# A convolution over 256 positions as products of 32-point transforms, eight graphs at a time, in a graph layer on one Trainium2 core

## The chip, the core and the metric

The kernel runs on one core of a Trainium2 chip. The time is device time in microseconds (us), the median of several runs. The core's engines work side by side, each through its own list of instructions in order: TensorE (PE), which multiplies matrices into PSUM, VectorE (DVE), ScalarE (ACT), GpSimd (POOL) and SyncE (SP). SP does nothing here but issue transfers (DMA) between device memory and the on-chip memory SBUF. An instruction whose operands another engine makes waits for it on a semaphore, and everything behind it on its engine waits too.

## The reference

There are 64 graphs of 256 nodes with 256 channels, all in fp32. With `h = relu(layernorm(x))` as its input, the layer computes:

```
xc = transpose(h)                                  # channels x nodes
c  = relu(bn1(conv1d(xc, conv1_w, pad 0)))         # 256 -> 256 channels, one tap
c  = bn2(conv1d(c, conv2_w, pad 8))                # 256 -> 256 channels, 17 taps along the nodes
x_conv = transpose(relu(c + xc))
s = h @ w_se.T + b_se                              # 3 numbers a node
A = exp(-squared distance of the s) * adj          # 256 x 256 a graph
x_nmp = A @ relu(h @ w_msg.T + b_msg)
r, z = sigmoid of sums of [x_conv, x_nmp] @ w_ih and h @ w_hh
n = tanh(gi_n + r * gh_n)
out = x + (1 - z) * n + z * h
```

Of all matmul work, conv2 with its 17 taps is the largest piece, and the gates (`w_ih`, `w_hh`) come second.

## The kernel before

The loop runs over 32 groups of `G` = 2 graphs. Channels lie on the 128 partitions (two halves, `DC` = 2), and the 512 nodes of a group along the free dimension. For each group, `norm` normalises on DVE (with a power on POOL), `transpose_h` turns the result on PE and ACT writes the relu `HT`. `conv1` multiplies, and ACT writes `H1`. `embed`, `message` and `affinity` make the adjacency part; POOL multiplies the exponential with `adj` (L324). `transpose_a` and `aggregate` follow, then `gates` for each half of the channels (`dc`), with four sums in PSUM, and `finish` transposes back, adds x and stores.

Conv2 is done in a short fast form along the nodes: `points` evaluates the input at seven points on DVE, `conv2` multiplies with filters that were evaluated at the same points at the start (seven points, five or four terms, 68 matmuls of 128x128 for each half of the output), and DVE puts four outputs together from the sums (L295 to L307). The node order in SBUF is chosen so that the pieces are contiguous.

The order is written out by hand in the loop at the end (`manual_schedule`): each engine takes its instructions in the order in which the code issues them. Buffers come from pools; a tile with `bufs=1` is written again only when all its readers are done. PSUM has eight buffers of 128x512: four `aux`, four `acc`. All loads and stores in the loop go through SP.

Of the kernel before, what the change touches and what calls it, by code (L numbers as in the profile page):

```python
# [1 line left out]

# [11 lines left out]
BN_EPS = 1e-5  # L14


@with_exitstack
def kernel(
# [30 lines left out]
    NP = B // G  # L49
# [16 lines left out]

    const = ctx.enter_context(tc.tile_pool(name="const", bufs=1))
    loads = ctx.enter_context(tc.tile_pool(name="loads", bufs=2))
    psum = ctx.enter_context(tc.tile_pool(name="psum", bufs=4, space=bass.MemoryType.PSUM))
# [4 lines left out]
    def rows(t, i, h):  # L74
        return t[G * i:G * i + G].rearrange("g (k h c) d -> h k g (c d)", c=MC, h=2)[h]
# [9 lines left out]
    X, ADJ = {}, {}  # L85

    def load(i):
        X[i] = loads.tile([P, G * MC, D], FP, name="x", bufs=3)
        ADJ[i] = loads.tile([P, G * MC, N], FP, name="adj")
        for t, src in ((X[i], x), (ADJ[i], adj)):  # L90
            for h in range(2):
                nc.sync.dma_start(out=t[h * NK:(h + 1) * NK].rearrange("k (g c) d -> k g (c d)", g=G),
                                  in_=rows(src, i, h))

    load(0)


# [11 lines left out]
    def fold_bn(params, name):  # L109
# [7 lines left out]
        nc.vector.tensor_sub(shift, b, shift)  # L117
        return scale, shift

    w_c1 = const.tile([P, DC, D], FP)  # L120
    nc.scalar.dma_start(out=w_c1, in_=c1_wT.rearrange("(k p) o -> p k o", p=P))
# [9 lines left out]
    nc.scalar.dma_start(out=w_msg, in_=msg_wT.rearrange("(k p) o -> p k o", p=P))  # L131
    b_msg = const.tile([P, D], FP)
    nc.gpsimd.dma_start(out=b_msg, in_=bass.AP(tensor=msg_b.tensor, offset=msg_b.offset, ap=[[0, P], [1, D]]))
    stage_ctx = ExitStack()
    stage = stage_ctx.enter_context(tc.tile_pool(name="stage", bufs=1))
    w_c2 = stage.tile([P, DC, TAPS, D], FP)
    for k in range(DC):
        nc.scalar.dma_start(out=w_c2[:, k], in_=c2_wT[k * P:(k + 1) * P])

    w_pt = const.tile([P, 2 * len(PTS), DC, L, D], FP)  # L140
    w_inf = const.tile([P, DC, L - 1, D], FP)
    for k in range(DC):
        taps = w_c2[:, k, :(L - 1) * F, :].rearrange("p (l j) o -> p j l o", j=F)
        nc.scalar.copy(w_inf[:, k], taps[:, F - 1])
        for q, a in enumerate(PTS):
            norm_a = 2 * a
            for b in PTS:
                if b != a:
                    norm_a *= a * a - b * b
            ev = stage.tile([P, L - 1, D], FP, name="ev", bufs=2)  # L150
            od = stage.tile([P, L - 1, D], FP, name="od", bufs=2)
            nc.vector.scalar_tensor_tensor(ev, taps[:, 2], a * a, taps[:, 0], op0=ALU.mult, op1=ALU.add)
            nc.vector.scalar_tensor_tensor(od, taps[:, 3], a * a, taps[:, 1], op0=ALU.mult, op1=ALU.add)
            nc.scalar.mul(ev, ev, 1.0 / norm_a)
            nc.scalar.mul(od, od, a / norm_a)
            nc.vector.tensor_add(w_pt[:, 2 * q, k, :L - 1, :], ev, od)
            nc.vector.tensor_sub(w_pt[:, 2 * q + 1, k, :L - 1, :], od, ev)
            nc.scalar.mul(w_pt[:, 2 * q, k, L - 1, :], w_c2[:, k, TAPS - 1, :], 1.0 / norm_a)
            nc.scalar.mul(w_pt[:, 2 * q + 1, k, L - 1, :], w_c2[:, k, TAPS - 1, :], -1.0 / norm_a)
    stage_ctx.close()  # L160
    work = ctx.enter_context(tc.tile_pool(name="work", bufs=1, reuse_waits="tile"))
# [4 lines left out]
    s2, h2_shift = fold_bn(bn2, "bn2")  # L166
# [3 lines left out]
    nc.vector.tensor_scalar(b_rz, b_rz, 0.5, None, ALU.mult)  # L170


    LD = const.tile([P, W], FP, name="ld")
    RD = const.tile([P, W], FP, name="rd")
    nc.vector.memset(LD, 0.0)
    nc.vector.memset(RD, 0.0)
    nc.vector.memset(LD[64:64 + SE, :], -1.0)
    nc.vector.memset(RD[32:32 + SE, :], -1.0)

    H1 = const.tile([P, F, DC * G, EK], FP, name="h1")  # L180
    nc.gpsimd.memset(H1, 0.0)
# [286 lines left out]
```

## Time and profile before

| | us |
|---|---|
| median of 3 runs | 2827.28 |
| lowest, highest | 2826.51, 2827.72 |
| the profiled execution's own time | 2828.4 |
| its span, from first to last instruction | 2826.6 |
| mean granted clock of PE, share of full speed | 0.958 |

The profile is of one execution. Its span is what the views divide; 1.8 us of that execution's time lie outside it. Busy time is the time in which an engine had an instruction running. The chain that ended last is followed back from the last instruction, at each step to what released it. [...] An fp32 matmul shows as two instructions, and a transpose as one.

### The profile page before, as it was taken

The numbers are of one execution on the slowest core, as the hardware profiler recorded it, in microseconds if no ns is written. First come the engines' busy times: TensorE is split into PE (matmuls) and PEld (weight loads), VectorE is DVE, ScalarE is ACT, GpSimd is POOL, SyncE is SP. The second block draws the span as 40 slices with busy tenths as digits, with TensorE's granted clock in tenths as the row PEclk, the third lists the DMA queues.
The fourth block names the chain that finished last, engine by engine and source line by source line (L and its number), as shares of the span: only waits on it lengthen the run. The fifth ranks groups of instructions, "written<-read, shape, count | busy, mean of one in ns | idle before, by whom it ended". The sixth has DMA issues, their size and how long they took to land.

```text
span 2826.6 us, 31684 instructions
## 1 busy us (share of the span) xinstructions
PE 2589.7 (92%) x13440; PEld 1863.1 (66%) x13440; DVE 965.5 (34%) x2343; ACT 538.8 (19%) x923; POOL 348.3 (12%) x443
## 2 busy tenths in 40 slices
PE   0899999999999999999999999999999999999998
PEld 0676667766677766677766677766677766677665
DVE  4332432332323433323433323333323323323322
ACT  2112211112211112111122111122111122111121
POOL 2111001111011111011111011111011111011110
PEclk9899999999999999999999999999999999999998
DMA  4000000000000000000000000000000000000000
GB/s 143 8 23 0 23 23 23 23 17 7 23 23 23 23 8 16 23 23 23 23 1 23 23 23 23 23 1 23 23 23 23 23 1 23 23 23 23 8 1 15
DMA packets 29982, 59.87 MB, mean 21 GB/s; under 512 B 3696, under 2 KB 4208, under 8 KB 29584
## 3 DMA queue, kind: packets, MB, share of 16 engines
q1 hardware_dynamic: 27648, 50.34, 6.5%
q10 hardware_dynamic: 1632, 7.34, 0.8%
q8 instruction: 106, 1.74, 0.3%
q0 software_dynamic: 560, 0.16, 0.0%
q14 instruction: 36, 0.29, 0.0%
HBM read 41.05 MB, written 16.78 MB: 20 GB/s over the span
## 4 chain that ended last, share of the span: by engine, by line
PE 89%; DVE 4%; ACT 2%; issue 1%; POOL 0%; DMA 0%; ACTq 0%; DVEq 0%
PE acc L359 35%; PE acc L284 34%; PE aux L344 7%; PE acc L219 4%; PE aux L268 4%; DVE u L304 2%; PE aux L318 2%; PE aux L254 2%; ACT hT L213 1%; PE aux L388 1%; DVE u L307 1%; ACT aT L336 1%; ACT mb L292 0%; DVE u L306 0%; DVE sm L297 0%
## 5 line engine op out<-in xcount | busy, mean ns | idle before, releaser
L284 PE MATMUL acc<-xp,w_pt 128*128 128x128 f32 x7680 | 869.6, 274 | 0.0
L284 PEld LDWEIGHTS acc<-xp,w_pt 128*128 128x128 f32 x7680 | 866.9, 191 | 1.8
L359 PE MATMUL acc<-xnm,w_ih 128*128 128x512 f32 x768 | 360.9, 592 | 0.0
L359 PE MATMUL acc<-xcv,w_ih 128*128 128x512 f32 x768 | 360.9, 592 | 0.0
L359 PE MATMUL acc<-hT,w_hh 128*128 128x512 f32 x768 | 350.4, 592 | 0.0
L344 PE MATMUL aux<-aT,msg 128*128 128x256 f32 x512 | 199.5, 572 | 149.1 <-ACT aT L336 149.1
L378 POOL TENSOR_TENSOR d<-hT,nn 128x512 f32<-128x512 f32 x64 | 82.3, 1286 | 1592.7 <-ACT nn L372 1592.7
L344 PEld LDWEIGHTS aux<-aT,msg 128*128 128x128 f32 x512 | 151.7, 304 | 191.6 <-ACT aT L336 156.6
L359 PEld LDWEIGHTS acc<-xcv,w_ih 128*128 128x128 f32 x768 | 145.9, 190 | 183.7 <-issue 183.7
L359 PEld LDWEIGHTS acc<-xnm,w_ih 128*128 128x128 f32 x768 | 145.9, 190 | 183.7 <-issue 183.7
L359 PEld LDWEIGHTS acc<-hT,w_hh 128*128 128x128 f32 x768 | 145.9, 190 | 170.0 <-issue 160.7
L368 DVE SCALAR_TENSOR_TENSOR gn<-tr,gn 128x512 f32<-128x512 f32 x64 | 44.1, 689 | 521.9 <-ACT tr L367 521.9
L379 DVE SCALAR_TENSOR_TENSOR d<-tz,d 128x512 f32<-128x512 f32 x64 | 44.3, 692 | 340.6 <-ACT tz L375 340.6
L295 DVE TENSOR_TENSOR sm<-acc,ma 128x256 f32<-128x256 f32 x64 | 27.2, 425 | 347.2 <-ACT ma L291 347.2
L297 DVE TENSOR_TENSOR sm<-acc,mb 128x128 f32<-128x128 f32 x64 | 18.7, 292 | 351.8 <-ACT mb L292 351.8
L284 PE MATMUL acc<-xp,w_inf 128*128 128x128 f32 x1024 | 124.8, 273 | 0.0
L272 POOL TENSOR_SCALAR msg<-msg 128x512 f32<-128x512 f32 x64 | 95.1, 1487 | 232.6 <-DVE msg L271 229.8
L324 POOL TENSOR_TENSOR a<-e,adj 128x128 f32<-128x128 f32 x256 | 123.5, 518 | 0.6 <-ACT e L321 0.6
L284 PEld LDWEIGHTS acc<-xp,w_inf 128*128 128x128 f32 x1024 | 119.5, 191 | 0.0
L219 PE MATMUL acc<-hT,w_c 128*128 128x512 f32 x256 | 117.1, 601 | 0.0
L268 PEld LDWEIGHTS aux<-w_msg,hT 128*128 128x128 f32 x512 | 97.3, 190 | 28.5 <-issue 16.9
L268 PE MATMUL aux<-w_msg,hT 128*128 128x256 f32 x512 | 115.7, 379 | 0.0
(89 smaller groups left out, 1921.3 us busy)
## 6 DMA issues: line engine op xcount, KB each, us to landing
x<-in_x_dram SPq DMA_DIRECT2D x64, 256.0 KB, 4.1
adj<-in_adj_dram SPq DMA_DIRECT2D x64, 256.0 KB, 4.8
out_dram<-y SPq DMA_DIRECT2D x64, 256.0 KB, 4.7
w_c<-in_c_wT_dram ACTq DMA_DIRECT2D x2, 2176.0 KB, 14.8
w_ih<-in_ih_wT_dram ACTq DMA_DIRECT2D x1, 1536.0 KB, 6.6
w_hh<-in_hh_wT_dram ACTq DMA_DIRECT2D x1, 768.0 KB, 8.4
w_c<-in_c_wT_dram ACTq DMA_DIRECT2D x1, 256.0 KB, 2.6
w_msg<-in_msg_wT_dram ACTq DMA_DIRECT2D x1, 256.0 KB, 6.0
```

What stands on the lines that cost most here:

```text
L219: nc.tensor.matmul(p, w_c1[:, k, o * P:(o + 1) * P], HT[i][:, k, :], start=(k == 0), stop=(k == DC - 1))
L254: nc.tensor.matmul(p[:KD, :], w_se[:, k, :], HT[i][:, k, :], start=(k == 0), stop=(k == DC - 1))
L268: nc.tensor.matmul(p[:, c * D:(c + 1) * D], chunk(HT[i][:, k], g, c), w_msg[:, k, :], start=(k == 0), stop=(k == DC - 1))
L272: nc.gpsimd.tensor_relu(MSG[i][:, g], MSG[i][:, g])
L284: nc.tensor.matmul(p, w[:, o * P:(o + 1) * P], XP[i][:, q, k * G:(k + 1) * G, l:l + NK], start=(l == 0 and k == 0), stop=(l == last - 1 an ...
L304: nc.vector.scalar_tensor_tensor(u[:, r // 2, r % 2], t[:, q], PTS[q] ** r, t[:, 0] if q == 1 else u[:, r // 2, r % 2], op0=ALU.mult, op1= ...
L318: nc.tensor.matmul(p[:, c * N:(c + 1) * N], chunk(LD[:KD], g, c), graph(RD[:KD], g), start=True, stop=True)
L324: nc.gpsimd.tensor_mul(AF_[i][:, g, c, b * P:(b + 1) * P].rearrange("p (h k) -> p h k", h=2), e[:, c, b * P:(b + 1) * P].rearrange("p (h k ...
L344: nc.tensor.matmul(graph(p, g), MSG[i][:, g, c, dc * P:(dc + 1) * P], AT[i][:, g, c, :], start=(c == 0), stop=(c == MC - 1))
L359: nc.tensor.matmul(p, w[:, row:row + P], r, start=(j == 0), stop=(j == len(terms) - 1))
L378: nc.gpsimd.tensor_sub(d, HT[i][:, dc, :], nn)
L379: nc.vector.scalar_tensor_tensor(d, tz, 1.0, d, op0=ALU.add, op1=ALU.mult)
```

## The change

Conv2 is computed through real transforms of 32 points, for `GB` = 8 graphs at a time (`PB` = 4 groups), in eight rounds.

The 256 nodes are cut into 16 windows of 16, and each output window needs the two neighbouring input windows. `split` forms sums (`U`) and differences (`V`) of them on DVE. The class `Fft` lists the steps of the transforms: `odd` on V, `even` on U. The way back is `odd_back`, `q_back`, `p_back` and `join`. A step is one DVE instruction on 256 to 2048 elements per partition, mostly in pieces of 16 elements; 20 small scalings go to ACT. The transforms leave 16 bins. For each bin `products` does three real products in place of a complex one (the last bin needs two): 4 matmuls of 128x128 each. Two bins go together, into three PSUM buffers, and DVE combines them into `Yv` or `Yu` (L562, L563).

The steps wait in a list, `queue`. `pump(us)` issues steps from it until an assumed length is used up, `drain` issues all that is left; the calls stand between the other parts of the loop and so set DVE's order.

The filters' transforms are computed at the start with the same steps, on DVE, one half of the input channels after the other, and written to device memory (`filt`, 16 bins of 768 KB, 512 KB for the last). Each round reads all of them again through SP into `wb`, which has three buffers.

Around it: `adj` now has one buffer; x is loaded a second time (`y`) through POOL, which also stores; DVE takes the product with `adj` (L617) and the subtraction that stood at L378; ACT takes relu and scalings of `message` and `embed`; PSUM has three `aux` and five `acc`. `gates` first adds what does not need conv2, then calls `middle`, then adds conv2's part. `residual` adds `HT` to all four groups' results ahead of the first gate's second part.

The core of the diff:

```diff
+    def odd(self, V, T, S):
...
+        q = [self.sub(T(None, 0, 2), V(None, 6, 2), V(None, 2, 2)),
+             self.add(T(None, 2, 2), V(None, 6, 2), V(None, 2, 2)),
+             self.stt(V(None, 6, 2), T(None, 0, 2), -R2, V(None, 4, 2)),
+             self.stt(V(None, 2, 2), T(None, 2, 2), -R2, V(None, 0, 2)),
+             self.stt(V(None, 4, 2), T(None, 0, 2), R2, V(None, 4, 2)),
+             self.stt(V(None, 0, 2), T(None, 2, 2), R2, V(None, 0, 2))]
...
+    def load_adj(i):
+        ADJ[i] = work.tile([P, G * MC, N], FP, name="adj")
+        load_rows(ADJ[i], adj, i, nc.sync)
...
+    filt = dram.tile([BINS, P, 3, DC, D], FP, name="filt")
+    def put(bins, kind, k, t):
+        nc.sync.dma_start(out=filt[bins:bins + t.shape[1], :, kind, k, :].rearrange("n p o -> p n o"), in_=t)
...
+        for s in fft.odd(V, T, Sv):
+            s()
+        for c in range(2):
+            put(c * 4, 0, k, V(c, 4, 4)[:, 0])
...
+        return psum.tile([P, W], FP, name="acc", bufs=5)
...
+    queue = deque()
+    def pump(us):
+        while queue and us > 0:
+            us -= queue.popleft()() / 960.0 + 0.1
+    def drain():
+        pump(1e9)
...
+    def split(j):
+        hv = h1.rearrange("p a (c h) b -> p (a c) h b", c=2)
+        A = slice(2 * G * j * DC, 2 * G * (j + 1) * DC)
+        for s, b in ((4, 0), (0, 1)):
+            a, bb = hv[:, :, s:s + 4, b:b + NW], hv[:, :, s:s + 4, b + 1:b + 1 + NW]
+            nc.vector.tensor_sub(V(None, s, 4)[:, A], a, bb)
+            nc.vector.tensor_add(U(None, s, 4)[:, A], a, bb)
...
+    def load_bin(b, n):
+        b, n = b + n // BINS, n % BINS
+        if b < NB:
+            WB[b, n] = work.tile([P, 3, DC, D], FP, name="wb", bufs=3)
+            kinds = 3 if n < BINS - 1 else 2
+            nc.sync.dma_start(out=WB[b, n][:, :kinds], in_=filt[n, :, :kinds])
...
+    def products(b, m):
+        load_bin(b, 2 * m + 2)
+        p = [acc() for _ in range(3)]
+        for n in range(2):
+            for kind, v in enumerate(operands(2 * m + n)):
+                if v is None:
+                    continue
+                for o in range(DC):
+                    for k in range(DC):
+                        nc.tensor.matmul(p[kind][:, (n * DC + o) * P:(n * DC + o + 1) * P],
+                                         WB[b, 2 * m + n][:, kind, k, o * P:(o + 1) * P],
+                                         v[:, k::DC, 0, :], start=(k == 0), stop=(k == DC - 1))
+        load_bin(b, 2 * m + 3)
+        p1 = work.tile([P, W], FP, name="p1")
+        pv = [t.rearrange("p (n a e) -> p a n e", n=2, e=NW) for t in (p1, p[1], p[2])]
+        if m < 7:
+            nc.scalar.copy(p1, p[0])
...
+            nc.vector.tensor_sub(re, pv[0], pv[2])
+            nc.vector.tensor_add(im, pv[0], pv[1])
...
+    def residual(i):
+        for o in range(DC):
+            v = xcv(i % PB, o)
+            nc.vector.scalar_tensor_tensor(v, v, s2[:, o:o + 1], HT[i][:, o, :], op0=ALU.mult, op1=ALU.add)
+            nc.scalar.activation(v, v, AF.Relu, bias=h2_shift[:, o:o + 1])
...
-    def conv2(i, o):
...
-        nc.scalar.activation(XCV[i][:, o, :], uf, AF.Relu, bias=h2_shift[:, o:o + 1])
...
+        for g in range(G):
             for c in range(MC):
-                for b in range(MC):
-                    nc.gpsimd.tensor_mul(AF_[i][:, g, c, b * P:(b + 1) * P].rearrange("p (h k) -> p h k", h=2),
-                                         e[:, c, b * P:(b + 1) * P].rearrange("p (h k) -> p h k", h=2),
-                                         ADJ[i][:, g * MC + c].rearrange("p (k h c) -> p c h k", h=2, c=MC)[:, b])
+                e = E[i][:, g, c].rearrange("p (c h b) -> p c h b", c=MC, b=NW)
+                nc.vector.tensor_mul(e, e, ADJ[i][:, g * MC + c].rearrange("p (b h c) -> p c h b", c=MC, b=NW))
+        if i + 1 < B // G:
+            load_adj(i + 1)
...
+    def gates(i, dc, middle=None):
...
+        pr, pn, pz = acc(), acc(), acc()
+        product(pr, h + xn, r, True, False)
+        product(pn, xn, n, True, False)
+        product(pz, h + xn, z, True, False)
+        if middle:
+            middle()
+        product(pr, xc, r, False, True)
         tr = work.tile([P, W], FP, name="tr")
         nc.scalar.activation(tr, pr, AF.Tanh, bias=b_rz[:, dc:dc + 1], scale=0.5)
         nc.vector.scalar_tensor_tensor(gn, tr, 1.0, gn, op0=ALU.add, op1=ALU.mult)
-        pn = product(xi, 2 * D + dc * P)
+        pump(1.5)
+        product(pn, xc, n, False, True)
...
+    def prepare(b, j, stats=True):
+        if b < NB:
+            i = b * PB + j
+            if stats:
+                norm(i)
+            transpose_h(i)
+            conv1(i)
+            split(j)
+            if i + 2 < B // G:
+                load_x(i + 2)
...
+    for b in range(NB):
+        i = b * PB
+        if b == 0:
+            queue.extend(fft.odd(V, T, Sv))
+            drain()
+            queue.extend(fft.even(U, PT, T))
+        products(b, 0)
+        pump(4)
         embed(i)
         message(i)
+        products(b, 1)
+        pump(5)
         affinity(i)
-        if i + 2 < NP:
-            load(i + 2)
-        conv2(i, 0)
-        if i > 0:
+        if b > 0:
             finish(i - 1)
-        if i + 1 < NP:
-            norm(i + 1)
-        conv2(i, 1)
-        if i + 1 < NP:
-            transpose_h(i + 1)
+        products(b, 2)
+        pump(6)
         transpose_a(i)
+        products(b, 3)
+        drain()
+        queue.extend(fft.odd_back(Yv, T))
         aggregate(i)
-        gates(i, 0)
-        if i + 1 < NP:
-            conv1(i + 1)
-            points(i + 1)
+        products(b, 4)
+        pump(6)
+        embed(i + 1)
+        message(i + 1)
+        products(b, 5)
+        pump(5)
+        affinity(i + 1)
+        queue.extend(fft.q_back(Yu, T))
+        products(b, 6)
+        pump(8)
+        if b + 1 < NB:
+            norm(i + PB)
+        transpose_a(i + 1)
+        products(b, 7)
+        queue.extend(fft.p_back(Yu, T))
+        queue.extend(fft.join(Yu, Yv, T))
+        aggregate(i + 1)
+        pump(8)
+        if b + 1 < NB:
+            transpose_h(i + PB)
+        embed(i + 2)
+        message(i + 2)
+        pump(5)
+        affinity(i + 2)
+        drain()
+        for j in range(PB):
+            residual(i + j)
+        def more(b=b, i=i):
+            if b + 1 < NB:
+                conv1(i + PB)
+                split(0)
+                if i + PB + 2 < B // G:
+                    load_x(i + PB + 2)
+            transpose_a(i + 2)
+        gates(i, 0, more)
         gates(i, 1)
-    finish(NP - 1)
+        aggregate(i + 2)
+        prepare(b + 1, 1)
+        gates(i + 1, 0)
+        embed(i + 3)
+        message(i + 3)
+        prepare(b + 1, 2)
+        finish(i)
+        gates(i + 1, 1)
+        affinity(i + 3)
+        gates(i + 2, 0)
+        transpose_a(i + 3)
+        prepare(b + 1, 3)
+        if b + 1 < NB:
+            queue.extend(fft.odd(V, T, Sv))
+            even = fft.even(U, PT, T)
+            queue.extend(even)
+        finish(i + 1)
+        gates(i + 2, 1)
+        aggregate(i + 3)
+        gates(i + 3, 0)
+        finish(i + 2)
+        gates(i + 3, 1)
+        while b + 1 < NB and len(queue) > len(even):
+            queue.popleft()()
```

Three places where the order of instructions matters. The first is DVE at the beginning of a round (from the second round on). Before, `message` was followed by conv2's sums:

```order
L271 TENSOR_TENSOR msg<-aux,b_msg 128x256 x4
L295 TENSOR_TENSOR sm<-acc,ma 128x256
L296 TENSOR_TENSOR df<-acc,ma 128x256
L297 TENSOR_TENSOR sm<-acc,mb 128x128
L298 TENSOR_TENSOR df<-acc,mb 128x128
```

Now the last odd step (into Sv) stands ahead of the first products' sums, and even steps (PT, U, T) stand between these, `message` and the product with `adj`:

```order
L62 TENSOR_TENSOR Sv<-V 128x2048
L562 TENSOR_TENSOR Yv<-p_1891,acc 128x16x32
L563 TENSOR_TENSOR Yv<-p_1891,acc 128x16x32
L62 TENSOR_TENSOR PT<-U 128x2048
L65 TENSOR_TENSOR U<-U 128x32x64
L602 TENSOR_TENSOR msg<-aux,b_msg 128x256 x4
L562 TENSOR_TENSOR Yv<-p_1952,acc 128x16x32
L563 TENSOR_TENSOR Yv<-p_1952,acc 128x16x32
```

The first of these rows is what PE's first products of the round read. The second place is SP. Before, its list in the loop held only x, `adj` and the output of a group:

```order
L92 DMA x_1535<-in_x_dram 64x2x512 x2
L92 DMA adj_1536<-in_adj_dram 64x2x512 x2
L393 DMA out_0_dram<-y_1634 64x2x512 x2
L92 DMA x_1943<-in_x_dram 64x2x512 x2
L92 DMA adj_1944<-in_adj_dram 64x2x512 x2
```

Now, at the beginning of the second round, it holds bins 2 to 5, the next `adj`, then bins 6 and 7:

```order
L522 DMA wb_1860<-filt_138 128x1536
L522 DMA wb_1889<-filt_138 128x1536
L522 DMA wb_1921<-filt_138 128x1536
L522 DMA wb_1950<-filt_138 128x1536
L303 DMA adj_1976<-in_adj_dram 128x1x512 x2
L522 DMA wb_1996<-filt_138 128x1536
L522 DMA wb_2025<-filt_138 128x1536
```

Bins 6 and 7 feed the fourth products, and the load of `adj` ahead of them waits until DVE has read the buffer. The third place is ACT at the first gate of a round. Before, conv2's last activation (`xcv`) stood some rows ahead of the gates:

```order
L308 ACTIVATE xcv<-u,bn_shift 128x512
L213 ACTIVATE hT<-aux 128x512 x2
L336 COPY aT<-aux 128x512 x2
L346 ACTIVATE xnm<-aux 128x512 x2
L364 ACTIVATE gn<-acc,b_hh 128x512
```

Now eight residual activations stand directly ahead of the gate's first read of PSUM, `gn`, and of conv1 for the next round:

```order
L580 ACTIVATE Yv_76<-Yv_76,bn2_shift_376 128x512 x8
L658 ACTIVATE gn_1243<-acc_1240,b_hh_385 128x512
L500 ACTIVATE h1_398<-acc_1258,bn1_shift_125,bn1_scale_124 128x2x16x16
L500 ACTIVATE h1_398<-acc_1262,bn1_shift_125,bn1_scale_124 128x2x16x16
L629 COPY aT_1273<-aux_1274 128x512
```

With five `acc` buffers, acc_1262 is the buffer that acc_1240 had, so the matmul that fills it comes after `gn`.

## Rows read from the trace of the kernel before

**Rows 1.** Page, section 1: engines, busy us, share of the span, instructions.
```profile
PE 2589.7 (92%) x13440; PEld 1863.1 (66%) x13440; DVE 965.5 (34%) x2343; ACT 538.8 (19%) x923; POOL 348.3 (12%) x443
```

**Rows 2.** Page, section 4: shares of the chain that ended last, by line.
```profile
PE acc L359 35%; PE acc L284 34%; PE aux L344 7%; PE acc L219 4%; PE aux L268 4%; DVE u L304 2%; PE aux L318 2%; PE aux L254 2%; ACT hT L213 1%; PE aux L388 1%; DVE u L307 1%; ACT aT L336 1%; ACT mb L292 0%; DVE u L306 0%; DVE sm L297 0%
```

**Rows 3.** The chain in order of time, 1400 to 1500 us: start, us, what.
```profile
1408.43 0.38 ACT mb L292
...
1414.80 6.17 PE aux L344 x16
1420.97 15.45 PE acc L359 x36
1436.42 3.43 PE acc L219 x8
...
1455.30 1.72 PE aux L254 x4
1457.02 3.45 PE aux L268 x16
1460.47 1.95 PE aux L318 x8
...
1477.61 0.87 PE aux L388 x8
1478.48 15.20 PE acc L284 x136
...
1493.71 0.38 ACT mb L292
```

**Rows 4.** Windows, same cycle: stretch, length, busy by engine, granted clock, DMA share, GB/s.
```profile
1380.00:1400.00 20.00, 20.00 (x182) 20.00 (x181) 7.60 (x25) 1.47 (x3) 1.38 (x3) 1.00 0.04 11
1414.80:1417.00 2.20, 2.20 (x5) 1.84 (x6) 0.00 (x0) 0.44 (x1) 0.00 (x0) 0.50 0.00 0
```

**Rows 5.** Groups by line and shape: busy us, mean ns, idle before.
```profile
L324 POOL TENSOR_TENSOR a<-e,adj 128x128 f32<-128x128 f32 x256 | 123.5, 518 | 0.6 <-ACT e L321 0.6
...
L271 DVE TENSOR_TENSOR msg<-aux,b_msg 128x256 f32<-128x256 f32 x128 | 47.5, 410 | 28.6 <-PE aux L268 28.6
...
L308 ACT ACTIVATE xcv<-u,bn_shift 128x512 f32<-128x512 f32 x64 | 46.2, 722 | 242.0 <-DVE u L307 242.0
...
L379 DVE SCALAR_TENSOR_TENSOR d<-tz,d 128x512 f32<-128x512 f32 x64 | 44.3, 692 | 340.6 <-ACT tz L375 340.6
...
L304 DVE SCALAR_TENSOR_TENSOR u<-df,u 128x128 f32<-128x128 f32 x128 | 37.4, 292 | 4.5
```

**Rows 6.** DVE's timeline in the tail of conv2: start us, us, what.
```profile
1409.04 0.28 DVE L298 TENSOR_TENSOR df<-acc,mb 128x128 f32<-128x128 f32 x1
1409.24 0.28 DVE L304 SCALAR_TENSOR_TENSOR u<-sm 128x128 f32<-128x128 f32 x1
1409.56 0.29 DVE L304 SCALAR_TENSOR_TENSOR u<-sm,u 128x128 f32<-128x128 f32 x1
```

**Rows 7.** Timeline of the start.
```profile
24.61 1.22 DVE L152 SCALAR_TENSOR_TENSOR ev<-w_c 128x1024 f32<-128x1024 f32 x1
...
68.12 0.43 DVE L196 BATCH_NORM_STATS2 st<-x 128x6 f32<-128x256 f32 x1
...
71.76 1.38 DVE L203 TENSOR_SCALAR xn<-x,mv,rstd 128x256 f32<-128x256 f32 x4 [1.21 <-POOL rstd L200]
...
79.89 1.88 PE L254 MATMUL aux<-hT,w_se 128*67 128x512 f32 x4
...
81.15 0.73 DVE L239 SCALAR_TENSOR_TENSOR eo<-h 128x544 f32<-128x544 f32 x1 [8.01 <-ACT h L222]
```

**Rows 8.** DMA issues: KB each, median us from issue to landing.
```profile
adj<-in_adj_dram SPq DMA_DIRECT2D x64, 256.0 KB, 4.8
...
w_c<-in_c_wT_dram ACTq DMA_DIRECT2D x2, 2176.0 KB, 14.8
w_ih<-in_ih_wT_dram ACTq DMA_DIRECT2D x1, 1536.0 KB, 6.6
```

More of the change, by code (lines that the diff above doesn't have):

```diff
@@ L82, in chunk, with load_rows, load_x, load_y @@
         return t[:, g * N + c * P:g * N + (c + 1) * P]
[L85 to L95, printed above, removed]
+    X, ADJ, Y = {}, {}, {}
+    def load_rows(t, src, i, eng):
+        for g in range(G):
+            eng.dma_start(out=row_tile(t, g), in_=rows(src, G * i + g))
+    def load_x(i):
+        X[i] = work.tile([P, G * MC, D], FP, name="x", bufs=2)
+        load_rows(X[i], x, i, nc.sync)
+    def load_adj(i):
+        ADJ[i] = work.tile([P, G * MC, N], FP, name="adj")
+        load_rows(ADJ[i], adj, i, nc.sync)
+    def load_y(i):
+        Y[i] = work.tile([P, G * MC, D], FP, name="y")
+        load_rows(Y[i], x, i, nc.gpsimd)
+    load_x(0)
+    load_x(1)
+    SL = GB * DC * L * NW
+    Ut, Vt, Yvt = (const.tile([P, SL], FP, name=n) for n in ("U", "V", "Yv"))
+    PTt, Svt, Tt = (const.tile([P, SL // 2], FP, name=n) for n in ("PT", "Sv", "T"))
+    fft = Fft(nc.vector, nc.scalar)
     ident = const.tile([P, P], FP)
@@ L160 @@
-    stage_ctx.close()
-    work = ctx.enter_context(tc.tile_pool(name="work", bufs=1, reuse_waits="tile"))
+        if k > 0:
+            w0 = load_taps(k)
+        U, V = (Slots(t, 1, L // 2, D) for t in (Ut, Vt))
+        PT, Sv, T = (Slots(t, 1, L // 4, D) for t in (PTt, Svt, Tt))
+        for c in range(2):
+            nc.scalar.copy(U(c, 0, 8), V(c, 0, 8))
+        e0 = w0[:, :D].rearrange("p (a n e) -> p a n e", a=1, n=1)
+        nc.vector.tensor_add(U(0, 4), V(0, 4), e0)
+        nc.vector.tensor_sub(V(0, 4), V(0, 4), e0)
@@ L196, in norm @@
             nc.vector.bn_stats(st[:, j, :], X[i][:, j, :])
+        for j in range(G * MC):
             nc.vector.bn_aggr(mv[:, j, :], st[:, j, :])
@@ L396 @@
-    load(1)
-    norm(0)
-    transpose_h(0)
-    conv1(0)
-    points(0)
-    for i in range(NP):
+                    nc.tensor.transpose(p[:, c * D + dc * P:c * D + (dc + 1) * P], chunk(OT[i, dc], g, c), ident)
+            nc.vector.tensor_add(row_tile(Y[i], g), p, row_tile(Y[i], g))
+            nc.gpsimd.dma_start(out=rows(out, G * i + g), in_=row_tile(Y[i], g))
+        if i + 1 < B // G:
+            load_y(i + 1)
+    def prepare(b, j, stats=True):
[8 more added lines that the diff above has]
+                load_x(i + 2)
@@ L426 @@
+    finish(B // G - 1)
 def kernel(**inputs):
```

449 lines of the change are left out of this document (300 added, 149 removed).

## The prediction

> **What bounds the kernel now.** I read the busy shares first. TensorE (PE) is busy 92% of a span of 2826.6 us [rows 1], and the chain that ended last lies on PE for 89%: 35% at L359, the gates, and 34% at L284, conv2 [rows 2]. So the other engines matter only where PE waits for them. The same chain in order of time shows one group of two graphs [rows 3]: from the end of one conv2 (ACT's copy L292 at 1408.43) to the end of the next (1493.71) it is 85.28 us, or 341.1 for eight graphs. In it PE works nearly all the time: 15.45 for each `gates`, 15.20 for each half of conv2 (136 instructions, 111.8 ns each; an fp32 matmul is two), 3.43 conv1, 1.72 embed, 3.45 message, 1.95 affinity, 0.87 for eight transposes. The one stall is the tail of conv2 on VectorE (DVE), after which `aggregate` needs 6.17 us for 16 instructions, where `message`, with 16 of the same width, needs 3.45. [...] I price every longer PE wait at this difference, 2.7 us, beside its own length.
>
> **What goes.** Conv2's 544 matmuls per eight graphs become 188 of the same 128x128 shape: 16 bins, three products each (two in the last), two output and two input halves. By the row's rate that is 188 x 2 x 111.8 ns = 42.0 us in place of 121.6, and PE's whole work for eight graphs is 4 x (30.9 + 3.43 + 1.72 + 3.45 + 1.95 + 3 x 0.87 + 3.45) + 42.0 = 232.0 us, if `aggregate` runs at the full clock. The difference to 341.1 is 109 us per eight graphs, 870 in all. That is the most the change can give; the question is what comes back as waits.
>
> **What comes: the transforms, on DVE.** Per eight graphs they are 39 steps with 20,480 elements per partition (odd half), 33 with 17,152 (even half) and 65 with 37,888 (way back). A DVE step of 128 elements takes 292 ns and one of 512 takes 692 [rows 5], so 1.04 ns an element; from start to start the fixed part is 0.07 us if the next step waits for nothing and 0.19 if it waits for this one [rows 6]. About half of the new steps wait, so I take 0.13 and keep both ends as bounds. Then the odd half is 26.4 us, the even half 22.2, the way back 47.9. The pieces that such a step reads are 16 elements long, shorter than any that the trace of before has on DVE (64); I take no extra for this, since the rows with pieces of 64 cost what whole rows cost, and put the other end among the rivals. DVE also takes over the adjacency product (POOL, L324, before) and L378.
>
> **The stretch from the first product to the first gate that needs conv2.** Here DVE is the longer side. In its order of instructions stand: even half 22.2, way back 47.9, 16 steps that bring the products out of PSUM 10.1, message and affinity 24 x 0.40 = 9.5, finish 1.3, norm 4 (5.0 at 68.12 to 73.14 [rows 7], one us of it filled), eight residual steps 5.3: 100.3 us. It also waits for PE:
> - at the first products, which run behind a wait, so at 5.36 + 2.7 = 8.1;
> - 3.0 at the second (embed, message and products, 10.5, against 7.5 on DVE);
> - 6.5 at the fourth: its filters stand on SP's queue behind the load of `adj`, which has one buffer and waits for DVE's affinity product, the last work that the buffer has. Behind it 512 KB of `adj` and 768 KB of filters must land, some 7 us between the rows for 256 KB (4.8) and 1536 KB (6.6) [rows 8], and then 8.1 of products at the low clock, against 8.9 of DVE work;
> - 5.4 at the fifth, which needs the last step of the even half, so that neither covers the other;
> - 2 each at the sixth and at the third message, which waits on ACT behind 14 scale operations.
>
> That is 27 us. Then ACT: the third matmul of conv1 (middle of `gates`) needs the PSUM buffer that ACT's `gn` frees, and this stands behind all eight residual activations; the last of them and `gn` add 1.4. PE resumes at 100.3 + 27 + 1.4 = 128.7 us. Its own work until there is products 42.0, embed and message 15.5, affinity 5.9, two `aggregate` 6.9, transposes 3.5, twelve of the first gate's 18 matmuls 10.3 and half of conv1 1.7, together 85.8: it has lost 43.
>
> **The stretch of the gates.** PE has 232.0 - 85.8 = 146.2 us left and is the longer side (DVE has 27.6 in the gates, 15 in three norms, 10.4 in split, the odd half and some 7 of smaller steps, 86). The waits: 2.7 for the clock after the one above. `prepare` now normalises directly ahead of PE's transposes, and DVE runs it behind the previous gates' last steps: ACT 0.7 (L308), two DVE steps 1.4 (L379) [rows 5], norm 5.0, ACT 0.6, together 7.7, less what PE has meanwhile. For j = 1 that is `aggregate`, 3.45: it loses 4.2 and half the clock price. For j = 2 norm stands behind the message steps, 0.8 + 5.0 + 0.6 = 6.4, plus 2.7. For j = 3 only one transpose lies between, 6.8 plus 2.7. With the first that is 26.9. At the end the next products need the last odd step. From the end of the last gate's first sum, 3.4 before PE's last matmul, the path is ACT 0.7, five gate steps 3.5, nine odd steps between them 4.3, nine behind them 3.6 and one of 2048 elements 2.3, so 14.4, and PE waits 11.0. Sum 146.2 + 26.9 + 11.0 = 184.1. A round of eight graphs takes 128.7 + 184.1 = 312.8, in place of 341.1.
>
> **Start and end.** Before, the loop begins at 79.9, and DVE's first filter step stands at 24.61, behind a small load that does not change [rows 7]. Then two passes over the filters, each 78 transform steps and subtractions with 41,984 elements, 54 us; between them 12 us, an estimate from the 4.8 us row, because the second pass's copy into U waits until SP has written 17 pieces of it; 3 us of small steps; four `prepare` in a row, each 13.0 from norm to the first step on conv1's output (68.12 to 81.15 [rows 7]) and 2.6 of split, 62.4; the odd half, 26.4. Together 24.6 + 54 + 12 + 54 + 3 + 62.4 + 26.4 = 236.4. The last round has no `prepare`: 214.8 of PE work, of which 84 are done when the first residual is ready at 120 (no norm, two residual steps in place of eight), so 130.8 remain, 2.7 for the clock and 8.4 for the last output: 262.
>
> **The sum.** 236.4 + 7 x 312.8 + 262 = 2688.0 us of span; 1.8 lie outside it in the profiled execution (2828.4 against 2826.6), and the runs' median is 1.1 below that one. I say 2689, 5% faster.
>
> Bounds: with 0.07 per step, no low clock and no wait behind `adj`, a round loses 9, 12 and 6 and is 286, the start is 224 and the last round 250: 224 + 7 x 286 + 250 = 2476. With 0.19, the low clock after the short waits too, and the affinity product at POOL's price (L324, 518 ns for 128, so 1.04 us for 256, against 0.41 for L271 [rows 5]; twelve on the path), a round gains 9, 5 and 8 and is 335, the start is 249 and the last round 280: 2874. For that product I take DVE's own row, since a step's cost follows its engine.
>
> [...] In before the strided read of `adj` lies on POOL, and no DVE row reads single elements 64 bytes apart, as L617 of the changed kernel does. [...]
>
> **Rivals.**
> - *PE stays the bound* (12%): the waits at the fourth and fifth product and in `prepare` are covered, as the lower bound has it. For it: DVE has only 186 of work against PE's 232. Against it: where its steps stand in order leaves PE nothing to do at those places. 2476 to 2600, about 2540.
> - *Filters' reads become the bound* (8%): 12.3 MB come in each round. At the rate of the 2176 KB row, 14.8 us [rows 8], a bin takes 5.3 and a pair 10.7, longer than a product and what lies between at the third and fourth; it adds some 5 us a round, 2729. Against it: 1536 KB landed in 6.6.
> - *Slower: 16-element pieces cost DVE extra* (14%). Path time in transform steps is 83 us a round and 136 at the start, 800 us in all; the 138 us that the sum gains are gone when such steps are 17% slower. At 25% it is 2889. For it: no row has such pieces. Against it: [rows 5], where 64-element pieces cost nothing.
>
> **How the numbers follow.** The walk above has 66%, with 2590 to 2790 as its own range. The range takes half of the first rival and the edge of the slower one: 2510 to 2860, some 82%. A difference under 0.2% can't be told from none here. Slower has nearly all of the last rival and the walk's upper edge, 16%; the same 2%; faster 82%.
>
> **What would show it.** L547 x3008 at 112 ns each; a round of 313 us between first products; PE waiting 13 us at the third conv1 matmul for ACT's `gn`; 11 at each round's first product for the last odd step, DVE's L62 into Sv; the fourth product waiting for a DMA into `wb`; first L547 at 236. Wrong would be: steps of 256 elements far from 0.41 us, PE waits at other places, or rounds at 232.

## The result and the profile after

The changed kernel takes 2675.34 us (median of 4 runs, 2673.58 to 2681.32) beside 2827.5 for the kernel before: a ratio of 0.9465, 95% interval [0.9448, 0.9481]. The forecast was 2689, 2510 to 2860. The profiled execution took 2674.03 us with a span of 2672.3. Of the four executions of the kernel "norm early" below, one took 3657 us at a granted clock of 0.568 and one 4266 us, for which a clock of 1.00 is on record, for reasons that stay open, so its numbers come from a second run.

The page's busy shares and the chain that ended last, by engine and by line, to set beside [rows 1, 2]:

```profile
PE 2026.6 (76%) x7744; PEld 1266.3 (47%) x7744; DVE 1485.3 (56%) x2641; ACT 635.4 (24%) x1077; POOL 127.6 (5%) x191
...
PE 62%; DVE 19%; issue 5%; DMA 5%; ACT 4%; POOL 1%; SPq 1%; DVEq 0%; POOLq 0%; ACTq 0%
PE acc L652 33%; PE acc L547 12%; PE acc L498 5%; DMA wb<-filt 5%; PE aux L599 4%; PE aux L637 2%; PE aux L491 2%; DVE T L62 2%; DVE e L617 2%; DVE V L59 2%; DVE Yv L65 2%; PE aux L586 2%; DVE T L65 1%; ACT Yv L580 1%; DVE V L65 1%
```

PE lost 563 us of busy time and the kernel gained only 152: the chain now leaves PE for 38% of its length. Conv2's share fell from 34% (L284) to 12% (L547); DVE's steps and the loads of `wb` came in.

The windows of the fourth round: the whole round, its stretch up to conv1's second output, and the stretch of the gates (columns: stretch, length, busy by engine, granted clock, DMA share, GB/s):

```profile
1151.94:1466.25 314.31, 254.66 (x968) 159.59 (x969) 172.77 (x309) 78.30 (x134) 13.83 (x20) 0.89 0.23 66
1151.94:1287.62 135.68, 97.77 (x553) 81.95 (x553) 94.93 (x161) 37.93 (x74) 3.48 (x5) 0.84 0.34 109
1287.62:1466.25 178.63, 156.90 (x416) 77.64 (x417) 77.84 (x148) 40.37 (x61) 10.36 (x15) 0.93 0.14 34
```

The walk had 312.8, 128.7 and 184.1. From one round's first product to the next it is 310.1, 309.8, 314.9, 314.3, 313.8, 310.6 and 310.6 us. PE is busy for 97.8 and DVE for 94.9 of the 135.7 us of the first stretch: they wait for each other in turn. PE's timeline of that round shows where (start, us, what, in brackets the idle time before it and what ended it; only the rows with over 2 us of it):

```profile
1151.94 2.04 PE L547 MATMUL acc<-Sv,wb 128*128 128x128 f32 x8 [9.80 <-issue]
...
1188.19 2.07 PE L547 MATMUL acc<-Sv,wb 128*128 128x128 f32 x8 [8.07 <-DMA wb<-filt]
...
1202.66 7.25 PE L547 MATMUL acc<-U,wb 128*128 128x128 f32 x48 [2.87 <-DVE U L62]
...
1238.98 2.08 PE L547 MATMUL acc<-U,wb 128*128 128x128 f32 x8 [9.13 <-DMA wb<-filt]
...
1255.33 5.20 PE L599 MATMUL aux<-w_msg,hT 128*128 128x256 f32 x16 [2.83 <-ACT hT L492]
...
1287.62 3.78 PE L498 MATMUL acc<-hT,w_c 128*128 128x512 f32 x4 [13.34 <-ACT gn L658]
...
1319.25 2.21 PE L491 MATMUL aux<-ident,x 128*128 128x128 f32 x8 [2.32 <-DVE x L482]
...
1351.00 2.10 PE L491 MATMUL aux<-ident,x 128*128 128x128 f32 x8 [4.44 <-DVE x L482]
...
1398.08 2.25 PE L491 MATMUL aux<-ident,x 128*128 128x128 f32 x8 [4.89 <-issue]
...
1466.25 2.04 PE L547 MATMUL acc<-Sv,wb 128*128 128x128 f32 x8 [10.07 <-issue]
```

The last row is the next round's; the nine above it are 57.7 us, where the kernel before had one such stall in each group of two graphs. (Two kinds of row say "issue": those at Sv begin when DVE's last odd step ends, at 1151.84 for the first, and the one at 1398.08 when L482's first does, at 1397.99.) Eight of the nine are in the prediction; the one at 1238.98, the eighth product, is not.

### The profile page after: what moved, and what is told of

Same layout as the page of the kernel before. It is cut to its first block, busy times and chain, and to the rows that moved or that the text cites. A ratio compares the mean times of both kernels' runs of the same rounds, so it can differ in the third digit from the quotient of the medians.

```text
span 2672.3 us, 20737 instructions
## 1 busy us (share of the span) xinstructions
PE 2026.6 (76%) x7744; PEld 1266.3 (47%) x7744; DVE 1485.3 (56%) x2641; ACT 635.4 (24%) x1077; POOL 127.6 (5%) x191
## 4 chain that ended last, share of the span: by engine, by line
PE 62%; DVE 19%; issue 5%; DMA 5%; ACT 4%; POOL 1%; SPq 1%; DVEq 0%; POOLq 0%; ACTq 0%
PE acc L652 33%; PE acc L547 12%; PE acc L498 5%; DMA wb<-filt 5%; PE aux L599 4%; PE aux L637 2%; PE aux L491 2%; DVE T L62 2%; DVE e L617 2%; DVE V L59 2%; DVE Yv L65 2%; PE aux L586 2%; DVE T L65 1%; ACT Yv L580 1%; DVE V L65 1%
## 5 line engine op out<-in xcount | busy, mean ns | idle before, releaser
L652 PE MATMUL acc<-Yv,w_ih 128*128 128x512 f32 x768 | 342.6, 596 | 8.7 <-ACT Yv L580 8.7
L491 PE MATMUL aux<-ident,x 128*128 128x128 f32 x256 | 62.3, 392 | 244.3 <-DVE x L482 210.1
L652 PEld LDWEIGHTS acc<-Yv,w_ih 128*128 128x128 f32 x768 | 146.5, 192 | 190.3 <-issue 180.9
L547 PE MATMUL acc<-U,wb 128*128 128x128 f32 x1024 | 145.0, 305 | 89.4 <-DMA wb<-filt 66.5
L547 PE MATMUL acc<-Sv,wb 128*128 128x128 f32 x512 | 84.0, 317 | 163.7 <-issue 68.9
L547 PEld LDWEIGHTS acc<-U,wb 128*128 128x128 f32 x1024 | 140.0, 219 | 95.4 <-DMA wb<-filt 68.4
L511 DVE TENSOR_TENSOR V<-h 128x512 f32<-128x512 f32 x64 | 44.1, 689 | 217.2 <-ACT h L500 217.2
L547 PEld LDWEIGHTS acc<-Sv,wb 128*128 128x128 f32 x512 | 76.6, 227 | 172.5 <-issue 74.5
L59 DVE SCALAR_TENSOR_TENSOR V<-T,V 128x256 f32<-128x256 f32 (+2 forms) x280 | 152.7, 609 | 0.2
L547 PE MATMUL acc<-V,wb 128*128 128x128 f32 x1024 | 145.4, 303 | 0.0
L547 PEld LDWEIGHTS acc<-V,wb 128*128 128x128 f32 x1024 | 141.4, 221 | 0.0
```

Of the source, the lines that this page charges most:

```text
L59: return self.step(out, lambda: self.v.scalar_tensor_tensor(out, x, s, y, op0=ALU.mult, op1=ALU.add))
L491: nc.tensor.transpose(chunk(p, j // MC, j % MC), X[i][:, j, dc * P:(dc + 1) * P], ident)
L547: nc.tensor.matmul(p[kind][:, (n * DC + o) * P:(n * DC + o + 1) * P], WB[b, 2 * m + n][:, kind, k, o * P:(o + 1) * P], v[:, k::DC, 0, :], ...
L652: nc.tensor.matmul(p, w[:, row:row + P], r, start=first and j == 0, stop=last and j == len(terms) - 1)
```

## The experiments

Each edit is made on the changed kernel unless the text says otherwise; ratios are to the kernel before, beside which each ran.

| kernel | median us | ratio | interval |
|---|---|---|---|
| changed kernel | 2675.34 | 0.9465 | 0.9448 to 0.9481 |
| adj behind the bins | 2527.67 | 0.8941 | 0.8928 to 0.8955 |
| gn first | 2614.77 | 0.9247 | 0.9225 to 0.9269 |
| norm early | 2551.81 | 0.9026 | 0.9013 to 0.9040 |
| adj read as it lies | 2655.12 | 0.9387 | 0.9371 to 0.9403 |
| extra work in the gap | 2653.31 | 0.9384 | 0.9370 to 0.9398 |
| first three together | 2361.48 | 0.8351 | 0.8338 to 0.8363 |
| and odd steps earlier | 2261.57 | 0.7999 | 0.7986 to 0.8012 |
| then two waits filled | 2357.23 | 0.8339 | 0.8325 to 0.8353 |
| norm for j = 0 alone | 2266.71 | 0.8018 | 0.8004 to 0.8031 |
| and filled, one residual ahead | 2262.11 | 0.8002 | 0.7990 to 0.8014 |
| and ACT's order changed | 2202.22 | 0.7783 | 0.7770 to 0.7796 |

**The place of the load of adj.** The theory under test is the walk: orders of instructions make PE wait. Its rivals say that PE's own work, or the rate at which filters come in, is the bound.

```
-        if i + 1 < B // G:
+        if i % PB > 1 and i + 1 < B // G:
             load_adj(i + 1)
...
         products(b, 3)
+        load_adj(i + 1)
...
         products(b, 7)
+        load_adj(i + 2)
```

> The load of adj moves behind the loads of bins 8 and 9, and the next one behind those of the next round's first bins; no size changes. The walk (the order of SP's queue makes PE wait): both DMA waits of a round (8.07 us at the fourth product, 8.1 to 9.1 at the eighth) go. DVE then sits idle 9.55 us less at the fourth and, since norm and the message steps follow closely, some 8.5 less at the eighth: 18 x 8 = 144 us, about 2531, between 2500 and 2550. Rival, the rate of the filters' reads is the bound: PE still waits there for wb, 2660 to 2680.

It took 2527.67, 148 less. Groups of lines (busy us, mean ns, idle before and what ended it), first of the changed kernel, then of this one:

```profile
L547 PE MATMUL acc<-U,wb 128*128 128x128 f32 x1024 | 145.0, 305 | 89.4 <-DMA wb<-filt 66.5 <-DVE U L62 23.0
```

```profile
L547 PE MATMUL acc<-U,wb 128*128 128x128 f32 x1024 | 134.4, 292 | 32.2 <-DVE U L62 32.2
```

The same bytes come in, and no row of L547 names `wb` any more. So it was the queue: bins 6 and 7, and 14 and 15, stood behind a load that waited for DVE. That decides against the filters' rate. PE's wait for the even half (U) grew from 2.87 to 4.08 us in a round, and a wait of 3.97 us for norm (L482) stands where it waited 2.83 for hT before.

**gn ahead of the residuals.**

```
         drain()
+        gn = hidden(i, 0)
         for j in range(PB):
             residual(i + j)
...
-        gates(i, 0, more)
+        gates(i, 0, more, gn)
```

Here `hidden` is what `gates` did first: the product ghn and ACT's read of it.

> The first gate's hidden product and its read gn stand ahead of the eight residual activations. The walk (conv1's second output waits for gn on ACT): the 13.3 us wait goes, conv1 and the transposes (5.6 us) are done before the first residual, and PE waits for that one instead; it resumes some 9 us earlier in seven rounds, 64 us, about 2611, between 2595 and 2630. Rival, DVE's way back sets the end of this stretch and the wait only moves: no change, 2665 to 2680.

2614.77, 61 less. The timeline of PE has one wait there, for the first residual:

```profile
1251.62 7.06 PE L661 MATMUL acc<-Yv,w_ih 128*128 128x512 f32 x12 [5.60 <-ACT Yv L580]
```

**norm one gates call earlier.**

```
         gates(i, 0, more)
+        early(b + 1, 1)
         gates(i, 1)
         aggregate(i + 2)
-        prepare(b + 1, 1)
+        prepare(b + 1, 1, False)
+        early(b + 1, 2)
         gates(i + 1, 0)
```

`early` calls `norm`; the same is done for j = 3.

> norm for j = 1, 2, 3 stands one gates call earlier in DVE's order. The walk: PE's three waits ahead of the transposes (2.3, 4.4 and 4.9 us) go, and with them most of 7.8 us of low clock behind them; I leave 3 us of it for the step from PE over ACT to PE: 16 x 7 = 112 us, about 2563, between 2540 and 2585. Rival, norm then delays the gates' own steps on DVE, so that nothing is won: 2660 or more.

The second run of the same kernel:

> The kernel of the run before last again (norm for j = 1, 2, 3 one gates call earlier), since that run's profile shows TensorE at a granted clock of 0.57 nearly all through, which no other run here does. The walk: a clock of 0.9, a time of 2540 to 2585 and no wait of PE for L482 in the stretch of the gates. Rival, the clock fell because of this order of the work: it falls again.

2551.81, 124 less (112 expected), with a clock of 0.913: this order of the work does not by itself lower the clock. PE's timeline at the place of the 2.32 us wait:

```profile
1263.66 1.04 PE L491 MATMUL aux<-ident,x 128*128 128x128 f32 x8
1265.00 3.70 PE L498 MATMUL acc<-hT,w_c 128*128 128x512 f32 x8 [0.30 <-ACT hT L492]
```

The transposes take 1.04 us in place of 2.21, for which the granted clock was 0.62: the wait and the low clock behind it went together.

**adj read as it lies.**

```
-  ADJ[i][:, g * MC + c].rearrange("p (b h c) -> p c h b", c=MC, b=NW)
+  ADJ[i][:, g * MC + c].rearrange("p (c h b) -> p c h b", c=MC, b=NW)
```

> The product with adj reads adj in the order in which it lies, so that the nodes of adj are not put in the right order (this changes the result); everything else is as it was. If single elements 64 bytes apart cost DVE extra, the mean of L617 falls from 587 ns to that of the message step, 417, and twelve of them lie on the path of a round: 12 x 8 x 0.17 = 16 us less, about 2659. Rival, its price is that of two SBUF operands and not of the stride: 587 stays, 2670 to 2680.

2655.12, 20 less. The line's own rows (ns min/median/max, first and last start), of the changed kernel and of this one:

```profile
L617 DVE TENSOR_TENSOR e<-e,adj x128: 575/586/601, 241.7 to 2593.9; 128x256 f32<-128x256 f32 x128
```

```profile
L617 DVE TENSOR_TENSOR e<-e,adj x128: 417/422/426, 242.9 to 2574.7; 128x256 f32<-128x256 f32 x128
```

So the stride costs 0.16 us a product, and the second SBUF operand is not what makes it dear.

**Extra work in the gap.**

```
+        if b + 1 < NB:
+            p = aux()
+            for j in range(10):
+                nc.tensor.matmul(p, w_c1[:, 0, :P], HT[i + PB][:, 0, :], start=True, stop=True)
```

> Ten extra matmuls of 512 columns, whose result nobody reads (8.6 us at the full clock), stand on PE in the 9.8 us in which it waits for the last odd step, in seven rounds. If the low clock behind a wait comes from PE standing still, the first product behind it falls from 7.5 to about 5.4 us: 2 x 7 = 14 us, about 2661. Rival, the clock falls whatever PE does, or the first product's time is set by something else: 7.5 stays, 2675, or a little more where the extra work ends late.

2653.31, 22 less. PE's timeline where a round begins:

```profile
1135.52 8.75 PE L800 MATMUL aux<-hT,w_c 128*128 128x512 f32 x20
1145.48 1.13 PE L547 MATMUL acc<-Sv,wb 128*128 128x128 f32 x8 [1.21 <-issue]
```

Its first product ends at 1150.91, 5.43 us after its start, where the changed kernel needs 7.52 (1151.94 to 1159.46). The windows of these two products, first of the changed kernel, then of this one (columns as above):

```profile
1151.94:1159.46 7.52, 7.52 (x49) 7.49 (x50) 0.00 (x0) 0.58 (x1) 0.00 (x0) 0.73 0.21 63
```

```profile
1145.48:1150.91 5.43, 5.43 (x48) 5.43 (x49) 0.00 (x0) 0.58 (x1) 0.00 (x0) 1.00 0.28 84
```

Work that nobody reads made the kernel faster by keeping the clock up, 1.00 in place of 0.73 here. Rounds are 2.9 us shorter on the mean (309.1 against 312.0). The first product is 2.1 of it; over seven rounds PE's busy time without the extra matmuls is 21 us less, so the rest is working time of PE too.

**The three together.**

> The first three edits together (adj behind the bins, gn first, norm early). They take 148, 61 and 123 us alone. If the waits lie one behind the other on one path, as the walk has them, the gains add: 2675 - 332 = 2343, between 2320 and 2375. Rival, they partly stand for the same wait, which returns elsewhere: 2400 or more.

2361.48, 314 less, so 18 us of the 332 do not come. No new wait took them: PE's longest waits apart from the round's end, 6.01 us for L580, 4.09 for U and 3.97 for L482, stand in the traces of the single edits too (5.60, 4.08 and 3.97). Over seven rounds PE's idle time falls by 221 us, where the three edits alone took 100, 55 and 72; its busy time, with the same 6768 instructions, falls by 75, where they took 33, 13 and 51. So most of what is missing is working time of PE. That edits had each won the same stretch of low clock would explain it; no run shows it.

**Odd steps earlier**, on top of the three: `prepare(b + 1, 3)` and the queue's filling move ahead of `gates(i + 2, 0)`, the norm for j = 3 moves ahead of `finish(i)`, one gates call earlier again, and the gates' pumps are 2.5, 2.5 and 4.5.

> As the three together, and prepare for j = 3 stands one gates call earlier, so that the odd steps can start some 15 us earlier, and the gates take 9.5 us of transform steps each in place of 6.5. The walk: the 9.8 us at a round's end with its low clock (12 us, seven rounds, 84) go, and some 13 us of the even steps leave the stretch in which DVE is the longer side, of which I count 8 a round (56): 2343 - 140 = 2203, between 2170 and 2260. Rival, longer pumps delay the gates' own steps and PE waits there: over 2300.

2261.57, 100 less where 140 were expected. The round's end has no wait any more, as the walk had it (84). If that gave its 84 in full, only 16 of the other 56 came. DVE's timeline in the first stretch:

```profile
1014.03 0.69 DVE L562 TENSOR_TENSOR Yv<-p,acc 128x512 f32<-128x512 f32 x1 [6.66 <-PE acc L547]
...
1022.84 0.69 DVE L562 TENSOR_TENSOR V<-p,acc 128x512 f32<-128x512 f32 x1 [7.53 <-PE acc L547]
```

Without the even steps DVE has nothing to do ahead of the fourth and fifth sums: there PE, which waits only 1.45 us at the fourth product and nothing at the fifth, has become the longer side.

**Filling two waits, three misses and a hit.** On top of that kernel:

```
-        if b + 1 < NB:
+        if b == 0:
             norm(i + PB)
...
             transpose_a(i + 2)
+            embed(i + 3)
+            message(i + 3)
...
+        early(b + 2, 0)
         gates(i + 3, 1)
```

> As the run before, and the two waits that its trace still shows in a round get work or lose their cause: embed and message of the fourth group stand on PE where it waits 6.0 us for the first residual (msg gets two buffers for it), and norm for j = 0 moves from the stretch in which DVE is the longer side into the last gates of the round before (PE waited 4.0 us for its L482). If what is left is waits on this path: 8.4 us with its low clock in eight rounds and 5 in seven, 2262 - 67 - 35 = 2160, between 2140 and 2200. Rival, PE now waits for the way back whatever stands ahead of it: over 2230.

2357.23, 96 more: two waits are new. The first stands on POOL, by its timeline:

```profile
1021.82 1.22 POOL L699 DMA_DIRECT2D out_dram<-y  x2 [34.08 <-DVE st L474]
1028.32 1.20 POOL L303 DMA_DIRECT2D y<-in_x_dram  x2 [5.28 <-issue]
1029.53 1.04 POOL L479 TENSOR_TENSOR rstd<-rstd,neg_half 128x4 f32<-128x4 f32 x1
```

DVE waits with it, by its own timeline:

```profile
1030.61 1.38 DVE L482 TENSOR_SCALAR x<-x,mv,rstd 128x256 f32<-128x256 f32 x4 [6.81 <-POOL rstd L479]
```

The second stands on PE:

```profile
1144.84 5.16 PE L599 MATMUL aux<-w_msg,hT 128*128 128x256 f32 x16 [12.39 <-ACT aT L629]
```

norm's power on POOL stood behind a load of y, and this behind the store out of the one buffer that y has (in the chain in order of time 4.21 us of that store stand ahead of the load, and in the trace of the next kernel POOL's loads of y wait 87.5 us in all for such stores). And message waited for PSUM that ACT's copies into aT free, behind eight residual activations. How the 96 us divide between the two was not separated.

The first edit alone, with `early(b + 2, 0)` ahead of `gates(i + 3, 0)`:

> As the kernel with prepare(b+1, 3) earlier (2262), with one edit of the last run alone and at another place: norm for j = 0 stands ahead of the first gate of the last group, where POOL has no load of y in front of its rstd that waits for a store. If that queue was why the last run lost (DVE waited 6.8 us for rstd, with the first products' sums behind it), PE's wait of 4.0 us for L482 and its low clock go, 5 x 7: 2227, between 2205 and 2245. Rival, norm in these gates delays the odd steps and with them the next round: 2262 or more.

2266.71, no gain. The 4 us for L482 went and came back as 3.79 for ACT's hT (behind 14 scalings) and 7.73 in place of 6.01 for L580. The second edit on top of it, with `residual` for j = 1 to 3 behind the first gate:

> As the one before, with the other edit of the run that lost: embed and message of the fourth group stand where PE waits for the first residual, and now only the first group's residual stands ahead of them (the other three behind the first gate), so that ACT's copies into aT, whose PSUM buffers message needs, wait for two activations in place of eight. If those eight were why PE waited 12.4 us there, 8 us in eight rounds go: 2227 - 64 = 2163, between 2140 and 2200. Rival, PE waits for the way back whatever stands ahead of it: 2215 or more.

2262.11, no gain. ACT's timeline at the first residual:

```profile
1093.28 1.33 ACT L580 ACTIVATE Yv<-Yv,bn_shift 128x512 f32<-128x512 f32 x2 [16.17 <-DVE Yv L579]
1094.52 1.43 ACT L500 ACTIVATE h<-acc,bn_shift,bn_scale 128x512 f32<-128x512 f32 x2
1095.85 1.06 ACT L629 COPY aT<-aux 128x512 f32<-128x512 f32 x2
```

and PE's:

```profile
1096.47 6.47 PE L599 MATMUL aux<-w_msg,hT 128*128 128x256 f32 x16 [8.44 <-ACT aT L629]
```

I had counted the activations in front of aT; but the first of them alone waits 16.17 us, and all behind it waits too. So the last edit moves it behind them:

```
         gn = hidden(i, 0)
-        residual(i)
...
             if b + 1 < NB:
                 conv1(i + PB)
-                split(0)
...
             transpose_a(i + 2)
             embed(i + 3)
+            residual(i)
+            if b + 1 < NB:
+                split(0)
...
             message(i + 3)
```

> As the run before (2262), with the first group's residual issued behind conv1, the transposes of a and embed, so that ACT's h1, aT, ld and rd stand ahead of its activations. There PE waited 8.4 us at message for ACT's aT, which stood behind an activation that waited 16 us for the way back. If ACT's order was the cause, message runs in that time and PE resumes the gate's second part with the first residual, some 8 us earlier in eight rounds: 2262 - 64 = 2198, between 2175 and 2215. Rival, the way back sets the end of this stretch in any order: 2250 or more.

2202.22, 60 less (64 expected), a ratio of 0.7783: the fastest kernel here, with the same operations as the changed one, apart from a second buffer for msg. PE's timeline there, where message no longer waits:

```profile
1065.49 3.62 PE L599 MATMUL aux<-w_msg,hT 128*128 128x256 f32 x16
1071.60 7.11 PE L661 MATMUL acc<-Yv,w_ih 128*128 128x512 f32 x12 [2.49 <-ACT Yv L580]
```

## Why the prediction was right

The mechanism is the one that was forecast; several sizes were off. The sum as measured is 217.2 for the start, 2184.0 for seven rounds (312.0 each) and 271.1 for the last, 2672.3, in place of 236.4, 7 x 312.8 and 262: the terms missed by -19, -6 and +9. Within a round errors cancel too: in the fourth, the first stretch is 7.0 us longer than in the sum and the stretch of the gates 5.5 shorter. That the total came within 0.5% is in part luck; what was right are the waits, eight of nine at their places.

- *Conv2's work.* L547 is there 3008 times. A product of 48 instructions that nothing delays takes 5.37 us, 111.9 ns each, as from [rows 3]; behind a wait it takes 8.16. The chain in order of time:

```profile
1164.63 5.37 PE acc L547 x48
...
1188.19 8.16 PE acc L547 x48
```

The difference is the 2.8 us that was priced at 2.7 from `aggregate`, where the granted clock is 0.50 at its start and 1.00 in conv2 [rows 4]; in the product of 8.16 it is 0.67, in that of 5.37 it is 1.00. Behind other waits of the round a product takes 7.25 (2.87 us of wait, for U) and 7.52 (9.80, for Sv), so 1.9 and 2.1 more: one price for all was too high there. That it is PE's standing still which costs it is shown by the extra work in the gap: 5.43 in place of 7.52, at a clock of 1.00 in place of 0.73.

- *A DVE step.* Pieces of 16 elements (16 and 32 in the second row) cost nothing extra, against [rows 5] with 410 and 692 (groups by shape from the first round on, columns as there):

```profile
L59 DVE SCALAR_TENSOR_TENSOR V<-T,V 128x256 f32<-128x256 f32 x112 | 39.3, 419 | 0.0
L59 DVE SCALAR_TENSOR_TENSOR T<-V 128x512 f32<-128x512 f32 x56 | 36.1, 685 | 0.2
```

In the rows below the same 16 steps take 5.45 us on the filters (from 42.45), where they read whole rows of 256, and 5.45 on the graphs (from 209.32), in pieces of 16. That takes the rival on the slower side away. The fixed part of 0.13 us was the mis-sized term: these steps are 0.34 from start to start, so it is 0.07 there, where a step does not read what the one ahead of it wrote. DVE's timeline of the start:

```profile
24.89 0.42 DVE L395 TENSOR_TENSOR U<-V,tr 128x256 f32<-128x256 f32 x1 [7.03 <-DMA tr<-in_c_wT_dram]
...
42.45 5.45 DVE L59 SCALAR_TENSOR_TENSOR V<-T,V 128x256 f32<-128x256 f32 x16
...
82.80 0.42 DVE L395 TENSOR_TENSOR U<-V,tr 128x256 f32<-128x256 f32 x1 [7.53 <-ACT U L393]
...
138.60 1.41 DVE L474 BATCH_NORM_STATS2 st<-x 128x6 f32<-128x256 f32 x4
...
151.87 1.40 DVE L474 BATCH_NORM_STATS2 st<-x 128x6 f32<-128x256 f32 x4
...
192.63 1.22 DVE L65 TENSOR_TENSOR T<-V 128x1024 f32<-128x1024 f32 x1
...
209.32 5.45 DVE L59 SCALAR_TENSOR_TENSOR V<-T,V 128x256 f32<-128x256 f32 x16
214.81 2.29 DVE L62 TENSOR_TENSOR Sv<-V 128x2048 f32<-128x2048 f32 x1
```

A pass takes 50.4 (24.89 to the idle 7.53 ahead of 82.80) in place of 54, the step between them 7.5 in place of 12, a `prepare` 13.3 in place of 15.6, the odd half 24.5 in place of 26.4.

- *The first stretch*, 135.7 in place of 128.7. DVE is busy 94.9, not 100.3: the same fixed part, while the twelve products with `adj`, busy 6.3 us where 4.8 were counted, went the other way. It is idle 40.8, not 28.4 (27 and the tail's 1.4), and its timeline has the misses:

```profile
1196.44 0.69 DVE L562 TENSOR_TENSOR Yv<-p,acc 128x512 f32<-128x512 f32 x1 [9.55 <-PE acc L547]
...
1210.02 0.69 DVE L562 TENSOR_TENSOR V<-p,acc 128x512 f32<-128x512 f32 x1 [7.42 <-PE acc L547]
...
1246.03 0.42 DVE L569 TENSOR_TENSOR V<-p,acc 128x256 f32<-128x256 f32 x1 [3.46 <-ACT p L566]
...
1258.85 0.76 DVE L602 TENSOR_TENSOR msg<-aux,b_msg 128x256 f32<-128x256 f32 x2 [4.56 <-PE aux L599]
```

The fourth product was counted at 6.5 and took 9.55, the fifth at 5.4 and took 7.42. The largest miss, 7.4 us, is the rule of the fourth product, applied once: `adj` is loaded again ahead of bins 14 and 15, PE's eighth product waits 9.13 us in the same way, and DVE waits 9.4 for its sums and the third message behind it, where 2 were counted. With adj behind the bins, the waits at the fourth, the eighth and this message are gone from DVE's timeline, and 7.41 at the fifth stay. The tail was right: PE waits 13.34 for gn, 13 forecast, and taking gn out of it gave 61.
- *The stretch of the gates*, 178.6 in place of 184.1. PE's three waits for norm are 11.7 us (2.3, 4.4 and 4.9, where 4.2, 6.4 and 6.8 were counted) and with their low clock 17.7, by what taking them out gave (124 us in seven rounds); 24.2 were counted for the three with it. The wait at the round's end was 10.07, 11.0 forecast.
- *The last round*, 271.1 in place of 262: it too has the wait at the eighth product, 8.5 us, and with adj behind the bins, which takes the fourth's as well, it is 254.1.
- *The stride of adj.* 586 ns against 422 without the stride are 0.64 ns an element more, and on the 1.04 of a plain step 1.68. That is 0.16 us a product, and 20 us in all. The sum had this price at nothing: it took 0.41 us for the product.
- *Filters' reads* fell with the first experiment. Its rate was off by a little, too: at 14.8 us for 2176 KB, 768 KB take 5.2 us and a pair 10.4, not 5.3 and 10.7.
- *PE stays the bound* fell: PE is busy 254.7 of 314.3 us. It is what the kernel comes nearer to when the orders are changed: rounds of 312.0 become 249 in the last kernel, against 232 of PE work.

## What to carry to other kernels

When work moves from one engine to another, write out each engine's order from the first instruction that needs the new work to the last, and ask at each step what stands ahead of it in the queue. Here that gave the time to 0.5%, in part by errors that cancel, while PE's saved work alone promised more than five times the gain. A wait found at one place of a pattern is to be looked for at each place where the pattern returns. And where an instruction waits long in an engine's list, all behind it waits too, so issue it behind all that is ready. Here three edits of orders without new work took the ratio from 0.9465 to 0.8351, and in ACT's list PE still waited 8.44 us with six residual activations fewer ahead of aT, while moving the last two behind it gave 60 us.

## What was not expected of the hardware

Matmuls without a purpose saved 22 us: behind them the first product of a round ran at a granted clock of 1.00 in place of 0.73. And a product that reads single elements 64 bytes apart cost 0.16 us more, for 256 elements, than one that reads them in a row (586 ns against 422).
